# Moving the tail work of the next blocks and the weight splitting in a fused retention and FFN kernel

## The chip, the cores and the metric

The kernel runs on one core of a Trainium2 chip. A core has TensorE (PE) for matrix products, VectorE (DVE), ScalarE (ACT) and GpSimd (POOL) for elementwise work, and SyncE (SP), from which this kernel issues nearly all of its DMAs. The engines run side by side, each through its own list of instructions in order, and wait for each other through semaphores. The metric is the device time in microseconds (us); lower is better.

## The reference

Input x is 4 x 1024 tokens of 512 features, float32. Two layers, each between a norm and a residual:

```python
x = x + layernorm(attn(layernorm(x)))
x = x + layernorm(ffn(layernorm(x)))

# attn, with 16 heads of 32 features and a decay lam per head
q, v = x @ Wq.T, x @ Wv.T
ret[t] = lam * ret[t-1] + v[t]            # along each sequence
out = layernorm(q * ret) * gamma + beta
out = (out * silu(x @ Wg.T)) @ Wo.T

# ffn, weights rounded to fp8, with 1536 hidden features
gate = silu((x @ gate_w) * gate_scale)
up = (x @ up_w) * up_scale
out = ((gate * up) @ down_w) * down_scale
```

## The kernel before, in words

The 4096 tokens are cut into 8 blocks of 512, each of 4 tiles of 128 tokens. Weights stay in SBUF or come through a ring of four buffers (`w_ring`), filled by DMA from SP: each product that has used a buffer issues the fetch for the product four later (`fetch_weights`).

The main loop (L1238) runs over t, the block whose FFN is computed, and i from 0 to 11, the slices of 128 hidden features. Every step (t, i) has three large groups of matmuls: `f.gate(i)` (pfg), `f.up(i)` (pfu) and `f.down(i - 2)` (pd). Between them, work of other blocks is laid in by hand:

- `b`, the retention layer of block t + 1: its products fill the gaps (pv, pq, pg and, for the output matrix, po), followed by moments, residual and norm.
- `n`, the retention layer of block t + 2: its x tiles are loaded, normed and turned.
- `l`, the tail of the FFN of block t - 1.

Each step has a first part (before `f.up`), a middle ("mid", after `f.fuse`) and an end. Everything is recorded through `InOrder` (L66 to L74), which keeps program order on each engine, so the position of a line in the loop is its position in the engine's list. All instructions carry line 74 in the profile; they are told apart by tile names. A step at which one engine waits holds up whatever stands behind it on that engine.

For b of block 2 and 3 the products are of the seven-product kind: `product` (L665) runs them in the orders at L333 to L336 (for the output: 1, 2, 6, 5, 3, 7, 4) on half matrices, in two PSUM banks, and VectorE or ScalarE adds each bank to a part in SBUF (`mids`). Number 6, 7 and 4 of a kind use one bank in turn, so number 4 of the output can accumulate only when VectorE has read number 7's sum (`add_o`, L733). The output products of every later block are of this kind too.

From block 4 on (`by_parts`) the v, q and g products use split weights and a split x. A weight is split into its upper bits (top), the rest (low) and a combination (diff); x likewise:

- `Splitter` (L395) prepares the weights in 12 units (v, q, g, four column chunks each) during t = 1 and 2. Unit n has a load (`l`, two DMAs), a split (`s`, three VectorE instructions and one of GpSimd) and a store (`k`, two DMAs), placed by the table `times` (L431). A unit uses a pair of 128 x 512 buffers: two pairs lie in the freed room of the output weights, and unit 7 has one under the tag xn.
- `low_of(k)` (L570) and `diff_of(k)` (L585) split tile k of x, with two VectorE instructions and one.
- x reaches its turned form through DRAM: `norm_x` (ScalarE), `send_x` (a VectorE transpose of 32 x 32 blocks and a DMA to `mx`), and `fetch_x` (L554, four DMAs; in these blocks once for tiles 0 and 1 and once for tiles 2 and 3).

For the retention block b, `o_moments(s)` takes mean and variance of the output of tile s (VectorE, then GpSimd for the root), `x1_of(s)` norms it (ScalarE) and adds the residual (GpSimd), `x1_moments(s)` and `x1n_of(s)` norm the sum, and `move_x1n(s)` or `turn_x1n(s)` turn it for the FFN. `center_y` (L845) subtracts the mean from y on VectorE, and ScalarE squares the result.

Of the kernel before, what the change touches and what calls it, by code (L numbers as in the profile page):

```python
# [10 lines left out]
F32 = mybir.dt.float32  # L11
# [6 lines left out]
P = 128  # L18
# [5 lines left out]
def retention_ffn_sandwich(  # L24
# [20 lines left out]
    NT, D = x.shape  # L45
    I = gate_w.shape[1]
    NC = D // P
    NI = I // P
# [10 lines left out]
    work = ctx.enter_context(tc.tile_pool(name="work", bufs=2))  # L59
# [6 lines left out]
    class InOrder:  # L66


        def __init__(self, engine):
            self.engine = engine  # L70
# [324 lines left out]
    class Splitter:  # L395


        def __init__(self):
            room = wpool.tile([P, 4, D], F32, tag="wo_sb", name="split_room")
            self.pairs = [(room[:, 0], room[:, 1]), (room[:, 2], room[:, 3])]  # L400
            self.units = [(k, c) for k in "vqg" for c in range(NC)]
            self.sources = {"v": wvT, "q": wqT, "g": wgT}
            self.pair = {n: p if p is None else self.pairs[p] for n, p in enumerate((0, 1, 0, 1, 0, 1, 0, None, 1, 0, 1, 0))}

        def load(self, n):
            k, c = self.units[n]
            if self.pair[n] is None:
                room = work.tile([P, 2, D], F32, tag="xn", name=f"split_room_{n}", bufs=1)
                self.pair[n] = room[:, 0], room[:, 1]
            w = self.pair[n][0]  # L410
# [15 lines left out]
        def store(self, n):  # L426
# [2 lines left out]
            sp.dma_start(operands[k, c]["low"], w)  # L429

        times = {  # L431
# [6 lines left out]
        }  # L438

        def at(self, *when):  # L440
# [664 lines left out]
    a = Retention(0, x_first)  # L1105
# [20 lines left out]
    b = Retention(1)  # L1126
# [111 lines left out]
    for t in range(NB):  # L1238
        f, n = Ffn(a), None
        fast = b is not None and b.fast  # L1240
        for i in range(NI):
            if t > 0 and (t > 1 or i) and not (fast and i == 11):
                (f if i else l).rest((i - 1) % NI)
            if t == 0 and i == 0:
                n = Retention(2)
# [40 lines left out]
                b.gap(3 * i)  # L1286
            if fast and 7 <= i < 10:
                b.product()
            if n and n.by_parts and i == 7:
                n.norm_x(1, True)  # L1290
                n.send_x(1)
            if n and n.by_parts and i == 8:
                n.fetch_x(1)
                n.low_of(0)
                n.low_of(1)
            if n and n.by_parts and i == 9:
                n.diff_of(0)
                n.diff_of(1)
            if t == PARTS - 2 and i == 9:
                for _ in range(RING - 1):  # L1300
                    fetch_weights()
# [48 lines left out]
            if fast and i == 9:  # L1350
                b.x1_moments(0)
                b.x1_moments(1)
            if fast and i == 10:
                b.x1_of(2)
                b.x1_of(3)
# [20 lines left out]
            if t == 0 and i == 11:  # L1376
                b.upper_of(2)
            if fast and i == 9:
                loads = []
                for s in range(2):  # L1380
                    b.x1n_of(s, shift_scale)
                    loads.append(b.move_x1n(s))
                for load in loads:
                    load()
                if n and not n.by_parts:
                    n.input_sums(1, 2)
# [36 lines left out]
            if fast and i in (7, 8):  # L1423
                b.product()
            if n and n.by_parts and i == 7:
                n.norm_x(2, True)
                n.send_x(2)
            if n and t > 0 and i == 8 and not n.by_parts:
                n.fetch_x()
            if fast and i == 8:  # L1430
                b.o_moments(0)
                b.o_moments(1)
                b.x1_of(0)
                b.x1_of(1)
            if fast and i == 9:
                b.o_moments(2)
                b.o_moments(3)
            if fast and i == 10:
                b.x1_moments(2)
                b.x1_moments(3)  # L1440
# [28 lines left out]
            if b and not fast and i >= 9:  # L1469
                b.rest_of(i - 9)  # L1470
            if n and t > 0 and i in (6, 7):
                for s in ([0], [3] if n.by_parts else [1, 2])[i - 6]:
                    n.norm_x(s, True)
                    n.send_x(s)
            for _ in range(look[i][1] if t == 1 else 0):
# [66 lines left out]
            if t == 1 and i == 0:  # L1542
                output_sums()
                splitter = Splitter()
# [9 lines left out]
            if b and i == 4 and 0 < t < NB - 2:  # L1554
                n = Retention(t + 2)
# [4 lines left out]
        l, a, b = f, b, n  # L1560
# [67 lines left out]
```

## Time and profile before

| What | Value |
|---|---|
| Time, median of 3 runs | 984.98 us (984.90 to 985.68) |
| Profiled execution | 984.96 us, of which its span is 983.1 us |
| Busy: TensorE, VectorE, ScalarE, GpSimd | 952.1, 681.0, 442.2, 270.8 us |
| DMA | 148.14 MB, mean 151 GB/s |
| One splitting unit on VectorE, undisturbed | 0.42 + 0.69 + 0.69 us |
| One pair of moments on VectorE (two tiles) | 1.7 us |
| Time between two blocks' same steps, t = 3 to 5 | 116.3 us |

Rows of a timeline give the start and duration in us, the engine, the line, the operation, its output and inputs, the shapes, how many instructions are merged, and in brackets the idle time of the engine before it with what ended it. Rows of a waits view give the total, the number of times and the longest. Starts are counted from the start of the span. TensorE's matmul ends are modelled, so distances between starts are safer than idle times.

### The profile page before, as it was taken

To read this page: it belongs to the slowest core of one execution; us is meant where nothing else is said; L and a number is where in the kernel's file an instruction comes from. 1 tells how busy PE (TensorE), PEld (TensorE's weight loads), DVE (VectorE), ACT (ScalarE), POOL (GpSimd) and SP (SyncE) were. 2 spreads that over 40 slices of the span, in tenths; PEclk is the share of its full clock that TensorE was granted. 3 is DMA by queue.
4 is the path that set the end of the run, shared out by engine and by line. 5 is a ranking of instruction groups with operands and counts; after the bars stand their busy time and mean duration, and the time that the engine had idled before them with its cause. 6 is when DMAs were issued, how large, how long until landed. Compare 5 with 4: busy or idle time off the path is not lost.

```text
span 983.1 us, 11900 instructions
## 1 busy us (share of the span) xinstructions
PE 952.1 (97%) x4022; PEld 746.2 (76%) x4022; DVE 681.0 (69%) x1042; ACT 442.2 (45%) x709; POOL 270.8 (28%) x340
## 2 busy tenths in 40 slices
PE   9999999999899998999999999999999999999997
PEld 7456766687787877878878788887878778787885
DVE  5996999767776888875577745876457755646445
ACT  3556675467566115343353424435263332625223
POOL 1405121403327134240332305222052212314020
PEclk9999999999999999999999999999999999999999
DMA  9311424845728666456455464556463464514021
GB/s 305 113 61 56 141 65 108 247 148 179 237 88 238 222 225 232 167 146 190 140 186 150 135 188 149 162 159 183 141 199 111 146 206 140 152 52 128 2 86 43
DMA packets 115756, 148.14 MB, mean 151 GB/s; under 512 B 10352, under 2 KB 61040, under 8 KB 115696
## 3 DMA queue, kind: packets, MB, share of 16 engines
q1 hardware_dynamic: 114832, 146.72, 48.3%
q8 instruction: 32, 0.52, 0.2%
q10 hardware_dynamic: 864, 0.66, 0.2%
q14 instruction: 28, 0.23, 0.1%
HBM read 108.81 MB, written 42.47 MB: 154 GB/s over the span
## 4 chain that ended last, share of the span: by engine, by line
PE 63%; DVE 18%; ACT 7%; POOL 5%; issue 4%; DMA 3%; SPq 0%; DVEq 0%; POOLq 0%; ACTq 0%
PE pfg L74 11%; PE pfu L74 10%; PE pd L74 10%; PE pv L74 8%; PE po L74 8%; PE pq L74 8%; PE pg L74 6%; DVE st L74 3%; ACT x1n L74 2%; DVE split_room L74 2%; DVE y L74 2%; DVE fuse L74 2%; DVE gate L74 1%; POOL x L74 1%; DVE scr L74 1%
## 5 line engine op out<-in xcount | busy, mean ns | idle before, releaser
L74 PE MATMUL pfu<-x1nT,up_sb 128*128 128x512 f32 x768 | 200.7, 403 | 7.1 <-DVE gate L74 7.1
L74 PE MATMUL pfg<-x1nT,gate_sb 128*128 128x512 f32 x768 | 195.4, 396 | 0.9 <-DVE x1nT L74 0.4
L74 PE MATMUL pd<-down_sb,fuse 128*128 128x512 f32 x720 | 184.8, 398 | 0.0
L74 PEld LDWEIGHTS pfu<-x1nT,up_sb 128*128 128x128 f32 x768 | 143.6, 188 | 43.1 <-DVE gate L74 10.9
L74 PEld LDWEIGHTS pfg<-x1nT,gate_sb 128*128 128x128 f32 x768 | 143.7, 188 | 32.9 <-ACT gate L74 2.1
L74 PEld LDWEIGHTS pd<-down_sb,fuse 128*128 128x128 f32 x720 | 136.1, 189 | 28.1
L74 ACT CAST fuse<-gate 128x512 fp32r<-128x512 f32 x90 | 55.7, 619 | 198.7 <-DVE gate L74 198.6
L74 ACT ACTIVATE gate<-pfg,gs_sb 128x512 f32<-128x512 f32 x96 | 65.6, 683 | 96.5 <-PE pfg L74 96.5
L74 DVE SCALAR_TENSOR_TENSOR gate<-pfu,us_sb,gate 128x512 f32<-128x512 f32 x96 | 71.6, 745 | 51.5 <-PE pfu L74 47.2
L74 POOL TENSOR_SCALAR mv<-mv 128x1 f32<-128x1 f32 (+1 forms) x82 | 24.3, 297 | 273.7 <-DVE mv L74 270.6
L74 DVE TENSOR_TENSOR fuse<-gate,fuse 128x512 fp32r<-128x512 f32 x90 | 74.7, 830 | 5.5 <-ACT fuse L74 5.5
L74 DVE BATCH_NORM_STATS2 st<-x 128x6 f32<-128x512 f32 x64 | 43.6, 681 | 24.8 <-POOL x L74 22.2
L74 POOL TENSOR_TENSOR ysum<-y 128x512 f32<-128x512 f32 (+1 forms) x10 | 11.8, 1183 | 171.2 <-DVE y L74 171.2
L74 POOL TENSOR_TENSOR mv<-mv,nhalf 128x1 f32<-128x1 f32 (+1 forms) x75 | 50.2, 670 | 6.2
L74 POOL TENSOR_TENSOR x<-x,x1n 128x512 f32<-128x512 f32 x32 | 41.5, 1296 | 12.3 <-ACT x1n L74 12.0
L74 POOL TENSOR_TENSOR d<-d,x 128x512 f32<-128x512 f32 x28 | 37.1, 1348 | 18.6 <-ACT d L74 16.7
L74 DVE TENSOR_TENSOR mids<-po,mids 128x512 f32<-128x512 f32 x30 | 20.5, 684 | 28.7 <-PE po L74 28.4
L74 POOL TENSOR_TENSOR sqsum<-sqsum,sq 128x512 f32<-128x512 f32 x24 | 34.9, 1454 | 17.4 <-ACT sq L74 16.0
L74 DVE TENSOR_TENSOR y<-pq,y 128x512 f32<-128x512 f32 x18 | 12.5, 692 | 37.4 <-PE pq L74 37.4
L74 POOL TENSOR_TENSOR ysum<-ysum,y 128x512 f32<-128x512 f32 (+1 forms) x20 | 22.2, 1110 | 52.1 <-DVE y L74 51.8
L74 DVE RECIPROCAL rstd<-rstd 128x512 f32<-128x512 f32 x8 | 26.8, 3352 | 11.5 <-ACT rstd L74 11.4
L74 ACT ACTIVATE scr<-scr,neg_low 128x1024 f32<-128x1024 f32 x18 | 20.6, 1145 | 24.1 <-DVE scr L74 24.0
(199 smaller groups left out, 1640.9 us busy)
## 6 DMA issues: line engine op xcount, KB each, us to landing
kept<-x SPq DMA_DIRECT2D x32, 256.0 KB, 2.5
x<-kept SPq DMA_DIRECT2D x32, 256.0 KB, 4.2
x<-in_x SPq DMA_DIRECT2D x28, 256.0 KB, 3.9
out<-d SPq DMA_DIRECT2D x27, 256.0 KB, 2.0
xnT<-mx SPq DMA_DIRECT2D x32, 128.0 KB, 2.9
w_ring_parts<-dtop_v SPq DMA_DIRECT2D x16, 256.0 KB, 3.0
w_ring_parts<-dlow_v SPq DMA_DIRECT2D x16, 256.0 KB, 3.3
w_ring_parts<-ddiff_v SPq DMA_DIRECT2D x16, 256.0 KB, 3.1
```

Source lines behind the costliest of these rows:

```text
L74: return lambda *args, **kwargs: tc.keep_in_program_order(op(*args, **kwargs))
```

## The change

Five things are moved, and two buffer pairs added. The splitting units: other places in `times`, with a third moment in a step ("start", before the up projection), and pairs also under the tags xn (units 7 and 11) and ret (unit 8). In blocks with `by_parts`: the second `fetch_x` goes from the start of step 8 to the end of step 7; `low_of` of tiles 2 and 3 from the end of step 8 to its middle, in front of the moments of output tiles 0 and 1; `diff_of` of tiles 0 and 1 from the start of step 9 behind the moments of x1 there. In every block with a fast b: `x1n_of` of tiles 0 and 1 in front of the fuse of step 9, and the moments of output tiles 2 and 3 in front of the turns of x1n in step 9. The regrouping of `norm_x` for tiles 2 and 3 leaves the order on each engine as it was.

```diff
             room = wpool.tile([P, 4, D], F32, tag="wo_sb", name="split_room")
-            self.pairs = [(room[:, 0], room[:, 1]), (room[:, 2], room[:, 3])]
+            self.pairs = {"a": (room[:, 0], room[:, 1]), "b": (room[:, 2], room[:, 3])}
...
-            self.pair = {n: p if p is None else self.pairs[p] for n, p in enumerate((0, 1, 0, 1, 0, 1, 0, None, 1, 0, 1, 0))}
+            places = ("a", "b", "a", "b", "a", "b", "a", "xn", "ret", "b", "a", "xn")
+            self.pair = dict(enumerate(places))
...
+            elif place == "ret":
+                self.pair[n] = [
+                    work.tile([P, D], F32, tag="ret", name=f"split_room_{n}_{h}") for h in range(2)
+                ]
...
         times = {
-            (1, 1, "end"): "l0 l1", (1, 2, "mid"): "s0", (1, 2, "end"): "k0", (1, 3, "mid"): "l2 s1",
-            (1, 3, "end"): "k1", (1, 4, "mid"): "l3 s2", (1, 4, "end"): "k2", (1, 5, "mid"): "l4",
-            (1, 8, "mid"): "s3", (1, 8, "end"): "k3", (1, 9, "mid"): "l5 s4", (1, 9, "end"): "k4",
-            (1, 10, "mid"): "l6", (2, 0, "mid"): "l7 s5", (2, 0, "end"): "k5 s6", (2, 1, "mid"): "l8 s7 k6",
-            (2, 1, "end"): "l9 s8", (2, 2, "mid"): "k7 k8 s9", (2, 2, "end"): "l10 k9", (2, 3, "mid"): "l11 s10",
-            (2, 3, "end"): "k10", (2, 4, "mid"): "s11", (2, 4, "end"): "k11",
+            (1, 1, "end"): "l0 l1", (1, 2, "mid"): "s0", (1, 2, "end"): "k0", (1, 3, "mid"): "l2",
+            (1, 3, "end"): "s1", (1, 4, "mid"): "k1", (1, 4, "end"): "l3", (1, 7, "end"): "s2",
+            (1, 8, "mid"): "k2", (1, 8, "end"): "l4 s3", (1, 9, "mid"): "k3 s4", (1, 9, "end"): "k4 l5",
+            (1, 10, "end"): "l6 l7", (2, 0, "start"): "s5 l8", (2, 0, "mid"): "k5 s6", (2, 0, "end"): "k6 l9 s7",
+            (2, 1, "start"): "s8", (2, 1, "mid"): "k7 l10 s9", (2, 1, "end"): "k8 k9 l11",
+            (2, 2, "end"): "s10", (2, 3, "mid"): "k10", (2, 3, "end"): "s11", (2, 4, "mid"): "k11",
         }
...
+            if (1, 0) < (t, i) < (2, NI):
+                splitter.at(t, i, "start")
...
             if n and n.by_parts and i == 8:
-                n.fetch_x(1)
                 n.low_of(0)
                 n.low_of(1)
-            if n and n.by_parts and i == 9:
-                n.diff_of(0)
-                n.diff_of(1)
...
             if fast and i == 9:
                 b.x1_moments(0)
                 b.x1_moments(1)
+                b.x1n_of(0, shift_scale)
+                b.x1n_of(1, shift_scale)
+                if n and n.by_parts:
+                    n.diff_of(0)
+                    n.diff_of(1)
...
             if fast and i == 9:
+                b.o_moments(2)
+                b.o_moments(3)
                 loads = []
                 for s in range(2):
-                    b.x1n_of(s, shift_scale)
                     loads.append(b.move_x1n(s))
...
+            if n and n.by_parts and i == 8:
+                n.low_of(2)
+                n.low_of(3)
             if fast and i == 8:
                 b.o_moments(0)
                 b.o_moments(1)
                 b.x1_of(0)
                 b.x1_of(1)
-            if fast and i == 9:
-                b.o_moments(2)
-                b.o_moments(3)
...
-            if n and n.by_parts and i == 8:
-                n.low_of(2)
-                n.low_of(3)
+            if n and n.by_parts and i == 7:
+                n.fetch_x(1)
```

More of the change, by code (lines that the diff above doesn't have):

```diff
@@ L399, in __init__ @@
             room = wpool.tile([P, 4, D], F32, tag="wo_sb", name="split_room")
-            self.pairs = [(room[:, 0], room[:, 1]), (room[:, 2], room[:, 3])]
+            self.pairs = {"a": (room[:, 0], room[:, 1]), "b": (room[:, 2], room[:, 3])}
             self.units = [(k, c) for k in "vqg" for c in range(NC)]
             self.sources = {"v": wvT, "q": wqT, "g": wgT}
-            self.pair = {n: p if p is None else self.pairs[p] for n, p in enumerate((0, 1, 0, 1, 0, 1, 0, None, 1, 0, 1, 0))}
+            places = ("a", "b", "a", "b", "a", "b", "a", "xn", "ret", "b", "a", "xn")
+            self.pair = dict(enumerate(places))
         def load(self, n):
             k, c = self.units[n]
-            if self.pair[n] is None:
+            place = self.pair[n]
+            if place == "xn":
                 room = work.tile([P, 2, D], F32, tag="xn", name=f"split_room_{n}", bufs=1)
                 self.pair[n] = room[:, 0], room[:, 1]
+            elif place == "ret":
+                self.pair[n] = [
+                    work.tile([P, D], F32, tag="ret", name=f"split_room_{n}_{h}") for h in range(2)
+                ]
+            else:
+                self.pair[n] = self.pairs[place]
             w = self.pair[n][0]
@@ L1425, in retention_ffn_sandwich @@
             if n and n.by_parts and i == 7:
-                n.norm_x(2, True)
-                n.send_x(2)
+                for s in (2, 3):
+                    n.norm_x(s, True)
+                    n.send_x(s)
             if n and t > 0 and i == 8 and not n.by_parts:
                 n.fetch_x()
+            if n and n.by_parts and i == 8:
+                n.low_of(2)
+                n.low_of(3)
             if fast and i == 8:
@@ L1471, in retention_ffn_sandwich @@
             if n and t > 0 and i in (6, 7):
-                for s in ([0], [3] if n.by_parts else [1, 2])[i - 6]:
+                for s in ([0], [] if n.by_parts else [1, 2])[i - 6]:
                     n.norm_x(s, True)
```

## The prediction

> **What bounds the kernel now.** I read the page first, then the waits of TensorE, then the timelines of TensorE, VectorE, ScalarE, GpSimd and the DMA queue around each wait. Steps are (t, i): t is the FFN block, i one of its twelve steps. The page:
>
> ```profile
> span 983.1 us, 11900 instructions
> PE 952.1 (97%) x4022; PEld 746.2 (76%) x4022; DVE 681.0 (69%) x1042; ACT 442.2 (45%) x709; POOL 270.8 (28%) x340
> ```
>
> TensorE sets the time. The change leaves TensorE's own list of instructions untouched, so only its gaps can change. The view of its waits gives them:
>
> ```profile
> PE pfu L74 <- DVE gate L74: 7.1, 9, 1.4
> PE pg L74 <- ACT mids L74: 5.8, 2, 2.9
> PE pt L74 <- DVE x1n L74: 3.7, 7, 1.2
> PE pq L74 <- DVE mids L74: 1.9, 2, 1.2
> ```
>
> The two long pg waits are in steps (1,4) and (2,4). In TensorE's timeline (start, duration; in brackets the idle time before):
>
> ```profile
> 246.77 2.18 PE L74 MATMUL pfu<-x1nT,up_sb 128*128 128x512 f32 x8
> 251.84 2.67 PE L74 MATMUL pg<-t_sums,w_ring 128*128 128x256 f32 x8 [2.90 <-ACT mids L74]
> ...
> 377.43 1.99 PE L74 MATMUL pg<-t_sums,w_ring 128*128 128x256 f32 x8 [2.86 <-ACT mids L74]
> ```
>
> Each gap costs about 3.05 us (the next start should be 248.8 and 374.4). After the first, the granted clock falls to half (third column from the right):
>
> ```profile
> 253.00:256.40 3.40, 3.40 (x9) 2.68 (x8) 1.85 (x3) 2.50 (x4) 2.56 (x3) 0.50 0.21 33
> ```
>
> That costs another 1.7 us. The reason for the wait stands in VectorE's timeline: a splitting unit in front of the subtraction of the mean from y, whose squares ScalarE needs before its mids.
>
> ```profile
> 242.92 0.42 DVE L74 TENSOR_SCALAR split_room<-split_room 128x512 int32<-128x512 int32 x1
> 243.37 1.67 DVE L74 TENSOR_TENSOR split_room<-split_room 128x512 f32<-128x512 f32 x1
> 245.08 1.65 DVE L74 SCALAR_TENSOR_TENSOR split_room<-split_room 128x512 f32<-128x512 f32 x1
> 246.65 2.47 DVE L74 TENSOR_TENSOR y<-y,mu 128x512 f32<-128x512 f32 x4
> ```
>
> In blocks t = 2 to 5 the same three waits recur; in block 3:
>
> ```profile
> 546.92 2.11 PE L74 MATMUL pfu<-x1nT,up_sb 128*128 128x512 f32 x8 [0.48 <-DVE gate L74]
> ...
> 554.02 2.14 PE L74 MATMUL pfu<-x1nT,up_sb 128*128 128x512 f32 x8 [0.95 <-DVE gate L74]
> ...
> 560.66 0.66 PE L74 MATMUL pt<-ident,x1n 128*128 128x128 f32 x4 [0.39 <-DVE x1n L74]
> ```
>
> Against the undisturbed rhythm (an 8-matmul group starts 1.81 us after the one before) these steps lose 0.65 + 0.29 + 1.25 + 0.58, with 0.38 of slow restarts: 3.15 us in a block.
>
> **What the Trainium skill says.** SBUF — State Buffer, "Who interferes with whom": a VectorE instruction with two SBUF inputs and a GpSimd one that reads SBUF exclude each other. The trace agrees: the split's passes take 0.69 alone and 1.67 and 1.65 above, beside GpSimd's d additions (243.07 to 246.18); top and low of tile 2 take 1.24 and 1.68 at 538.1 beside the x additions, 0.42 and 0.69 elsewhere. TensorE: Matmul & The Clock Gate, "Part 1: The HAM clock gate": an idle window of about 3.4 us, free-running, halves the clock. The trace shows 3.4 us at 0.50 after one of two such gaps. The table at the head of that page calls VectorE's and ScalarE's queues strict FIFO; nothing above contradicts it.
>
> **The change part by part**
>
> *Splitting units, (1,3) and (2,3).* The unit now stands behind y - mu. For (2,4): y - mu runs from 369.15, not 372.24; the third square's buffer waits for GpSimd's first sqsum addition, which follows two d additions of 1.28 each (start 368.66) and so ends near 372.6, not 375.7. Square 0.63, gate 0.67, mids 0.59: mids ends near 374.4, when TensorE wants it. 3.05 us go. What is late next: the split, now beside the three sqsum additions, takes about 4 us, then fuse, gate, half. half ends near 380.3, and var on TensorE would now start at 379.75: about 0.6 comes back. Gain 2.4. In (1,4) the same with 0.3 left of the first wait and 0.7 at var, plus the clock's 1.7: 3.05 + 1.7 - 1.0 = 3.7.
>
> *Units at the end of block 1.* The unit in step 8 goes behind the o addition, into 2.12 us of idle time; nothing. In step 9 the two o moments (1.72) move in front of the turns, where VectorE idled 2.03 + 1.04, and the x1n norms pass the fuse cast on ScalarE. gate of step 10 then ends near 312.1 instead of 312.85: the wait of pfu 11 falls from 1.57 to 0.8, limited by the split beside GpSimd's t_sums. x1n 2 and 3 come 1 to 2 us earlier, so that pt's 0.6 goes. Gain 1.4.
>
> *SP's queue.* Load 5 reuses pair b and waits for store 3 to land (issued near 312, landing after 4.4 as the stores do at 313): the queue stands until about 316.5. Behind it are two kept stores, three copies of 1.95 in all, loads 6 and 7 (1.0 each). The weight fetch that went out at 321.17 goes out near 323.4; it took 5.6 to land there. Its product is at 329.32, minus the 1.4: 327.9. Stall between 0 and 1.6; I take 0.5.
>
> *Block 2, steps 0 to 2.* One more unit in front of gate in step 1 (two more by then, 1.77 each, one in 1.46 of idle time): gate at 343.9 instead of 341.9, so the copy of the first q product ends at 345.8, and the third q product (345.27) waits 0.6. In exchange the later unit is gone and the fifth q product's wait (1.36 at 353.74) falls away. Gain 0.7.
>
> *low of tiles 2, 3.* The heart of the matter, in t = 2 to 5. The four instructions (2.12 us) now stand in front of the o moments and of the addition for the sixth o product (number 7). They need the second xnT fetch, which SP can't issue earlier, since it waits for the x tiles' store to land. In block 3 it is issued 531.48 to 533.28 and the last part lands 3.8 after 532.83: 536.6. VectorE comes there at 534.6 and stands, with everything behind it. low to 538.8, two moments 1.7, the addition 0.7: 541.2. Before, that addition was here:
>
> ```profile
> 537.47 0.69 DVE L74 TENSOR_TENSOR mids<-po,mids 128x512 f32<-128x512 f32 x1 [1.12 <-PE po L74]
> ```
>
> and the last o product, which accumulates in the bank that it reads, follows close behind:
>
> ```profile
> 539.10 1.89 PE L74 MATMUL po<-w_ring_parts,y 128*128 128x256 f32 x8
> ```
>
> So a new wait of 2.1 us. By the landings the others are 2.7 (t = 2), 2.5 and 2.4, a mean of 2.4; I take off 0.1, as the dtop fetch no longer goes in front, and add 0.15 for the restart: 2.45. (gate 9 of ScalarE ends near 544.0, before pfg 10 at 546.6: no second wait.) What goes: after a delay of 2.45, gate of steps 9 and 10 end near 547.6 and 551.9 against wants of 548.4 and 554.0, x1n 3 likewise early; all 3.15 us go. Net 0.7, times four: 2.8. But gaps of 2.2 to 2.7 are near those of which one in two halved the clock; I count one of the four: -1.7. Net 1.1. No cover means here: each us by which xnT lands later costs 4 us in all.
>
> *Block 6.* No new loads. Moments 4 us earlier, the x1n norms 2 us: pt's 1.05, the start's 0.28 and pfg's 0.38 at 908.89 go. Gain 1.6 with restarts, less 0.1.
>
> *diff of 0 and 1 behind the x moments; the second unit in 2,4:* VectorE does them in time already counted.
>
> Sum: 3.7 + 2.4 + 1.4 - 0.5 + 0.7 + 1.1 + 1.5 = 10.3. The profiled execution took 984.96 around its span of 983.1 (1.86 outside it), the median is 984.98. 984.96 - 10.3 = 974.7.
>
> **Rivals.** (A) xnT lands sooner than in the profile (536.0 in block 3's time) and no clock drop: the new wait is 1.5, four blocks give 1.5 each, most of the residues at var and the late fetch go: 6.0 + 4.3 + 2.9 + 1.4 + 0.7 + 1.5 = 16.8, 968.2. For it: the dtop fetch is out of the way. Against: the wait for the store stays. (B) The splitting units' gain is taken by the next waits: var on half, the third q product and the late fetch (1.6) keep half of it: 2.7 + 1.0 + 0.7 - 1.6 + 0 + 1.1 + 1.0 = 4.9, 980.1. For it: VectorE is busy without a break from 329.6 to 342.7. (C) Slower: low of tile 2 waits long in all four blocks, and the gap halves the clock each time. The parts outside it give 9.2; so it decides from a loss of 2.8 in a block (2.3 to level, 0.5 for the bound): a wait of about 4.1 with the clock's 1.7, which means a landing 1.8 us later than now. With 2.5 us later: 4 x (4.95 - 3.15 + 1.7) = 14, less 9.2: 989.8. For it: landings of 5.6 occur at 321. Against: the xnT parts land after 2.5 to 3.8. (D) Nothing happens since the waits only change places: 984.
>
> **How the numbers follow.** Forecast (971 to 978) 0.5, A 0.17, B 0.17, C 0.12, D 0.04. Changes under 0.2% (2.0 us) can't be told from none. Faster: 0.5 + 0.17 + 0.17 = 0.84; same 0.04; slower 0.12. Range 967.5 to 984: it takes in A and B and leaves C and the tail of A out.
>
> **What would show it.** Right: no pg wait over 1 us on mids, no 0.50 clock near 253; a new wait "po from DVE mids" four times, 2 to 2.7 each; pfu on gate gone in t = 2 to 6; VectorE's top waiting for the DMA of xnT. Wrong: no such po wait (then A), waits of var and pq over 1 us (B), po waits over 4 with the clock at 0.50 (C).

## The result and the profile after

| | Median | Runs | Ratio to before, 95% interval |
|---|---|---|---|
| before | 985.05 us | 984.90 to 985.68 | |
| changed | 975.81 us | 974.44 to 976.66 | 0.9904 [0.9887, 0.9921] |

The changed kernel is 9.2 us faster; 974.7 was forecast. Its profiled execution took 975.05 around a span of 973.3, which is 9.8 us less than the span before. The page, after the change:

```profile
span 973.3 us, 11904 instructions
PE 948.2 (97%) x4022; PEld 745.0 (77%) x4022; DVE 677.3 (70%) x1042; ACT 442.5 (45%) x709; POOL 275.6 (28%) x340
```

TensorE has the same 4022 matmuls as before, so the 9.8 us can only come from gaps and from its clock. The view of its waits shows where the gaps went (total, times, longest):

```profile
PE po L74 <- DVE mids L74: 7.7, 4, 2.3
PE pfu L74 <- DVE gate L74: 1.6, 1, 1.6
PE pv L74 <- DVE total L74: 1.2, 1, 1.2
...
PE mu L74 <- ACT half L74: 0.7, 1, 0.7
```

The two pg waits (5.8) are gone, eight of the nine pfu waits too, and of pt's seven waits one is left (1.1, in block 0, as before). In their place stand four po waits, which the prediction had announced as "four times, 2 to 2.7 each" (they are 1.0 to 2.3); a pv wait at the start of block 2, which it had put at 0 to 1.6; and mu in (2,3), which it had not announced. Here mu and var are TensorE's products for the mean and the variance of y, fed by `half`, and pt are the turns of x1n.

TensorE's timeline at the two places where pg had waited 2.9 us, which now has no idle time in brackets:

```profile
245.32 2.18 PE L74 MATMUL pfu<-x1nT,up_sb 128*128 128x512 f32 x8
247.33 1.94 PE L74 MATMUL pg<-t_sums,w_ring 128*128 128x256 f32 x8
...
370.23 1.94 PE L74 MATMUL pg<-t_sums,w_ring 128*128 128x256 f32 x8
...
533.17 1.99 PE L74 MATMUL po<-w_ring_parts,y 128*128 128x256 f32 x8 [1.04 <-DVE mids L74]
...
540.45 1.98 PE L74 MATMUL pfu<-x1nT,up_sb 128*128 128x512 f32 x8
...
545.89 1.98 PE L74 MATMUL pfu<-x1nT,up_sb 128*128 128x512 f32 x8
```

The last three lines are block 3: one new wait at the last output product, and behind it both up projections of steps 10 and 11 on time. VectorE in (1,3) shows the reordering, with y minus the mean first and the splitting unit behind it:

```profile
242.14 2.48 DVE L74 TENSOR_TENSOR y<-y,mu 128x512 f32<-128x512 f32 x4 [0.59 <-PE mu L74]
244.53 1.25 DVE L74 TENSOR_SCALAR split_room<-split_room 128x512 int32<-128x512 int32 x1
245.82 1.67 DVE L74 TENSOR_TENSOR split_room<-split_room 128x512 f32<-128x512 f32 x1
247.52 1.65 DVE L74 SCALAR_TENSOR_TENSOR split_room<-split_room 128x512 f32<-128x512 f32 x1
...
644.55 0.43 DVE L74 TENSOR_SCALAR top<-xnT 128x512 int32<-128x512 int32 x1 [2.51 <-DMA xnT<-mx]
...
648.30 0.66 DVE L74 TENSOR_TENSOR mids<-po,mids 128x512 f32<-128x512 f32 x1
```

The last two lines are the origin of the po waits, here in block 4: VectorE stands 2.51 us for the second xnT fetch, and the addition that frees the bank of the last output product runs only at 648.30, behind low and two moments. In this block the clock then fell to half. Busy times by window (third column from the right is the granted clock); the second window follows the po wait of block 5, which was nearly as long (2.39 us from start to start, against 2.70) and had no such effect:

```profile
649.24:652.65 3.41, 3.41 (x9) 2.66 (x9) 0.32 (x2) 2.33 (x5) 3.23 (x3) 0.50 0.18 67
766.00:769.40 3.40, 3.16 (x14) 2.75 (x15) 1.91 (x4) 2.77 (x6) 3.30 (x4) 1.00 0.03 11
```

**Where the time went.** Since the order of TensorE's matmuls is the same in both kernels, each start of before can be set against the start of the same matmul after. The advance grows or shrinks at these places:

| Place | Forecast | Measured |
|---|---|---|
| step (1,4) with the clock | +3.7 | +4.0 |
| end of block 1 | +1.4 | +0.2 |
| late weight fetch, block 2 step 0 | -0.5 | -1.35 |
| block 2, steps 0 to 2 | +0.7 | +0.8 |
| mu in (2,3) | not in the sum | -1.1 |
| step (2,4) | +2.4 | +2.5 |
| blocks 2 to 5, with one clock drop | +1.1 | +1.7 |
| block 6 | +1.5 | +1.4 |
| one pq wait in block 1 | not in the sum | +0.9 |
| first 60 us (a start-up phase) | none | +0.6 |

The last two rows can't be put down to the change: the start-up phase moves by about 1 us between other pairs of kernels below, and at this pq product kernels whose program is the same up to there have 0.25 to 1.30 us from start to start. The rows add up to 9.7; the rest are shifts under 0.2 each.

### The profile page after: what moved, and what is told of

It reads as the page before. It is cut to its first block, busy times and chain, and to the rows that moved or that the text cites. A ratio compares the mean times of both kernels' runs of the same rounds, so it can differ in the third digit from the quotient of the medians.

```text
span 973.3 us, 11904 instructions
## 1 busy us (share of the span) xinstructions
PE 948.2 (97%) x4022; PEld 745.0 (77%) x4022; DVE 677.3 (70%) x1042; ACT 442.5 (45%) x709; POOL 275.6 (28%) x340
## 4 chain that ended last, share of the span: by engine, by line
PE 65%; DVE 15%; DMA 5%; POOL 5%; ACT 4%; issue 4%; SPq 1%; DVEq 0%; ACTq 0%; POOLq 0%
PE pfg L74 12%; PE pfu L74 12%; PE pd L74 11%; PE pv L74 9%; PE pq L74 8%; PE po L74 6%; PE pg L74 5%; DVE st L74 3%; DMA mx<-xn 2%; DVE y L74 2%; DVE split_room L74 2%; DVE fuse L74 1%; DMA xnT<-mx 1%; SPq L74 1%; DVE half L74 1%
## 5 line engine op out<-in xcount | busy, mean ns | idle before, releaser
L74 POOL TENSOR_TENSOR mv<-mv,nhalf 128x1 f32<-128x1 f32 (+1 forms) x75 | 53.1, 709 | 6.2
```

The lines of the kernel that those rows point to most:

```text
L74: return lambda *args, **kwargs: tc.keep_in_program_order(op(*args, **kwargs))
```

## Experiments

Times are medians; each ratio is to the kernel before, run beside it on the same chip. "Matched starts" means the comparison just used. A wait in brackets is idle time of TensorE; a gap "start to start" runs from one matmul's start to the next one's and is about 0.4 longer.

| Kernel | Median us | Ratio, 95% interval |
|---|---|---|
| splitting units alone | 979.63 | 0.9953 [0.9938, 0.9967] |
| moments and x1n norms alone | 974.71 | 0.9902 [0.9886, 0.9919] |
| changed, low back at the end of step 8 | 970.84 | 0.9851 [0.9834, 0.9867] |
| changed, low behind the moments | 975.43 | 0.9906 [0.9880, 0.9933] |
| changed, low in step 9 | 971.86 | 0.9878 [0.9854, 0.9903] |
| the same, kept stores later | 966.86 | 0.9814 [0.9799, 0.9829] |
| changed, units 1 and 11 in front of y - mu | 985.05 | 0.9997 [0.9982, 1.0012] |
| all mends, low in step 9 | 964.06 | 0.9787 [0.9772, 0.9802] |
| all mends, low at the end of step 8 | 965.99 | 0.9806 [0.9791, 0.9820] |
| changed, again | 976.59 | 0.9906 [0.9884, 0.9928] |

**1. The two halves of the change, each alone.** The first takes from the change only the table of the units, its pairs and the third moment of a step:

```diff
-            self.pairs = [(room[:, 0], room[:, 1]), (room[:, 2], room[:, 3])]
+            self.pairs = {"a": (room[:, 0], room[:, 1]), "b": (room[:, 2], room[:, 3])}
...
         times = {
...
+            (1, 3, "end"): "s1", (1, 4, "mid"): "k1", (1, 4, "end"): "l3", (1, 7, "end"): "s2",
...
+            if (1, 0) < (t, i) < (2, NI):
+                splitter.at(t, i, "start")
```

> The kernel before with the new table and pairs of the splitting units alone; low, moments, x1n, fetch and diff as before. From the matched starts of the two traces the units' share is +4.2 in (1,4), -1.35 at the late weight fetch, +0.8 in block 2 steps 0 to 2, -1.1 at mu in (2,3), +2.5 in (2,4), together +5 us: 979 to 981 us, no po wait, the pfu waits of 7 us and the pt waits still there. Rival (the end of block 1 is held up by the units there, and the moments' move hides it in the full change): pfu waits at the end of block 1 of 2 us or more beyond those before; 982 to 984 us.

Measured: 979.63, 4.3 us faster than the kernel beside it. The pg waits are gone by matched starts (+3.1 in each step, and about 1.4 of the clock in (1,4)); mu costs 1.1. But the rival has a part in it. TensorE at the end of block 1:

```profile
308.56 3.31 PE L74 MATMUL pfu<-x1nT,up_sb 128*128 128x512 f32 x8 [2.72 <-DVE gate L74]
```

The wait there grew from 1.42 to 2.72, and the clock halved behind it, 2.9 us lost in all. In the full change the moments in front of the turns take that back: its wait is 1.61. The number met the theory in part by luck: the late weight fetch, counted at -1.35, cost nothing here, since TensorE comes to it later by what it lost at pfu.

The second half moves the moments of output tiles 2 and 3 in front of the turns and the x1n norms of tiles 0 and 1 in front of the fuse, and nothing else:

```diff
             if fast and i == 9:
                 b.x1_moments(0)
                 b.x1_moments(1)
+                b.x1n_of(0, shift_scale)
+                b.x1n_of(1, shift_scale)
...
             if fast and i == 9:
+                b.o_moments(2)
+                b.o_moments(3)
                 loads = []
                 for s in range(2):
-                    b.x1n_of(s, shift_scale)
                     loads.append(b.move_x1n(s))
...
-            if fast and i == 9:
-                b.o_moments(2)
-                b.o_moments(3)
```

> The kernel before with only the moments of output tiles 2 and 3 in front of the turns of x1n in step 9 and the x1n norms of tiles 0 and 1 in front of the fuse. Theory (this part frees pfu 11 and pt; low at the end of step 8 still delays gate 10 by its 2.1 us, which leaves the 0.65 of pfu 10): about 2.3 us in each of four blocks, 1.4 in block 6, 1 to 2 at the end of block 1: 972 to 975 us, with pfu waits of some 2 us left and no pt waits. Rival (the moments alone bring nothing as long as low stands at the end of step 8, since gate 10 is late either way): 982 to 985 us.

Measured: 974.71, 9.2 us faster, as much as the whole change. TensorE's waits (dlow_v is the low part of the v weights in DRAM):

```profile
PE pg L74 <- ACT mids L74: 5.8, 2, 2.9
PE pfu L74 <- DVE gate L74: 1.8, 4, 0.5
PE pv L74 <- DMA w_ring_parts<-dlow_v: 1.7, 3, 0.8
```

The theory held: 2.1 to 2.35 us a block by matched starts (pfu 11 1.25, pt 0.6 to 0.7, the rest at pfg 11), 1.2 in block 6, 1.6 at the end of block 1, where the pfu wait is gone, and four short waits of pfu 10 are left, which low at the end of step 8 causes. The third line is new: three waits for a weight fetch, of which more below. The moments and the x1n norms were not tried apart, so their shares stay open.

The halves sum to 13.5 us and the whole brought 9.2, so the remaining part, which is mainly the place of low, should cost about 4.

**2. Low back at the end of step 8.**

```diff
-            if n and n.by_parts and i == 8:
-                n.low_of(2)
-                n.low_of(3)
             if fast and i == 8:
                 b.o_moments(0)
...
             if fast and i in (7, 8):
                 b.product()
+            if n and n.by_parts and i == 8:
+                n.low_of(2)
+                n.low_of(3)
```

> The changed kernel with low of tiles 2 and 3 back at the end of step 8; the fetch, diff, moments and x1n norms stay where the change put them. From the two halves of the change (units alone 4.3 us, moments alone 9.2 us faster than before, the whole change 9.2), the move of low would cost 4.3 us. Theory (the halves add up, low in the middle of step 8 is a loss): 970.5 to 973 us, no po waits, pfu 10 waits of about 0.4 in four blocks. Rival (the halves overlap, and each bought part of the same time): 974.5 to 977 us even without the po waits, with other waits in their place.

Measured: 970.84, ratio 0.9851 against 0.9904 for the change, and the intervals don't touch. The move of low was a loss of about 5 us inside a gain. Its waits for gate and for dlow_v:

```profile
PE pfu L74 <- DVE gate L74: 3.3, 5, 1.6
PE pv L74 <- DMA w_ring_parts<-dlow_v: 2.5, 4, 1.1
```

The matched starts give the loss as a sum. From this kernel to the changed one, the po gaps cost 2.5 + 1.1 + 2.3 + 2.0 and the clock 1.8: 9.7 us. In return four pfu 10 waits of 0.5 go (1.9), and so do the four waits for dlow_v (3.7), since a TensorE that has just stood 2 us asks for that weight later. Net 4.1. More than a third of the new stall's price is hidden, because it stands in front of another stall that it makes unnecessary. In block 3, for example, the fetch goes out at 549.64 in this kernel and at 549.89 in the changed one, but TensorE asks for it at 552.97 here and at 554.12 there. The gain with low back is 14 us, about what the two halves sum to, so the moves of the second `fetch_x` and of diff are worth little either way.

**3. What makes the po wait: the landing or the work?** One kernel puts the moments of tiles 0 and 1 in front of low, so that they fill the time in which VectorE stands; the other takes low out of step 8.

```diff
+            if fast and i == 8:
+                b.o_moments(0)
+                b.o_moments(1)
             if n and n.by_parts and i == 8:
                 n.low_of(2)
                 n.low_of(3)
             if fast and i == 8:
-                b.o_moments(0)
-                b.o_moments(1)
                 b.x1_of(0)
```

> In step 8 of blocks 2 to 5 the moments of output tiles 0 and 1 (1.7 us) stand in front of low of tiles 2 and 3, so that they fill the time in which VectorE stands for the second xnT fetch. Theory (the landing wait, with moments and number 7's addition queued behind it, makes the four po waits of 1.0 to 2.3 us): the po waits sum to 1 to 2 us in place of 7.7, the clock drop at 649 goes (1.7), the later waits of pfu 10 stay away; 969 to 972 us, 0.4 to 0.7% faster than the changed kernel. Rival (the amount of work in front of the addition makes it late, since low and moments together are 3.8 us in either order): the po waits stay near 7.7 in sum and the time near 975.8.

Measured: 975.43, the same as the change within the intervals, where the theory wanted 969 to 972. The profiled execution itself took 971.43, the others 975.17 to 977.78, and only the profiled one left a trace. In it three of the four po waits had shrunk to gaps of 0.34 to 0.45 start to start (0.23 is the rhythm), as the theory has it. In block 2 the wait had grown to 2.9, with the clock at half behind it, and VectorE shows a cause that neither side had named:

```profile
414.28 0.43 DVE L74 TENSOR_SCALAR top<-xnT 128x512 int32<-128x512 int32 x1 [0.90 <-DMA xnT<-mx]
414.75 0.69 DVE L74 TENSOR_TENSOR low<-xnT,top 128x512 fp32r<-128x512 f32 x1
415.36 1.51 DVE L74 TENSOR_SCALAR top<-xnT 128x512 int32<-128x512 int32 x1
416.91 1.63 DVE L74 TENSOR_TENSOR low<-xnT,top 128x512 fp32r<-128x512 f32 x1
418.46 0.68 DVE L74 TENSOR_TENSOR mids<-po,mids 128x512 f32<-128x512 f32 x1
```

GpSimd at that time:

```profile
414.77 3.22 POOL L74 TENSOR_TENSOR x<-x,x1n 128x512 f32<-128x512 f32 x2 [0.34 <-ACT x1n L74]
```

Earlier moments release the x additions on GpSimd earlier, and low now runs beside them: top and low of tile 3 take 3.14 us in place of 1.11. The Trainium skill says of this in SBUF — State Buffer, section "Who interferes with whom", that a VectorE instruction with two SBUF inputs and a GpSimd one that reads SBUF hold each other up; the trace agrees, with 0.69 alone and 1.63 beside. Whether this, or a late landing, also made the slower executions of this kernel can't be told. So the run shows that the landing makes the wait in three blocks, and does not show a gain from this order.

The other kernel:

```diff
-            if n and n.by_parts and i == 8:
-                n.low_of(2)
-                n.low_of(3)
...
             if fast and i == 9:
                 b.o_moments(2)
                 b.o_moments(3)
+                if n and n.by_parts:
+                    n.low_of(2)
+                    n.low_of(3)
                 loads = []
```

> low of tiles 2 and 3 moves from step 8 to step 9, behind the moments of output tiles 2 and 3 and in front of the turns of x1n. Theory (low at its place in step 8 costs its wait for the landing and gives nothing; all of the recovered 2.9 us per block comes from the moments in front of the turns and the x1n norms): no po waits, pfu 10 and 11 still without waits, 2.4 us per block in four blocks less than the changed kernel, and no drop of the clock at 649 (1.7): 964 to 967 us. Rival (it was low's leaving of the end of step 8, with 2.1 us less in front of gate 10, that freed step 10, so that low in step 9 gives the waits of pfu 10, pfu 11 or pt back): po waits gone, but 1.5 to 3 us of pfu and pt waits per block; 973 to 977 us.

Measured: 971.86 (970.11 to 975.22). The po waits are gone and pfu 10 and 11 are on time, so the rival falls: the place of low in step 8 gave nothing that step 9 doesn't give. But the forecast of 964 to 967 is missed by 5 us, because a third wait had stood behind both. TensorE in block 4:

```profile
664.25 1.11 PE L74 MATMUL pv<-xnT,w_ring_parts 128*128 128x512 f32 x4
666.78 1.19 PE L74 MATMUL pv<-low,w_ring_parts 128*128 128x512 f32 x4 [1.42 <-DMA w_ring_parts<-dlow_v]
```

and the DMA queue of SP before it:

```profile
658.90 1.54 SPq L74 DMA_DIRECT2D x1n<-mxs  x2
660.48 0.91 SPq L74 DMA_DIRECT2D kept<-x  x2
661.43 0.49 SPq L74 DMA_DIRECT2D w_ring_parts<-dlow_v  x1
```

The product that frees the buffer for this fetch is the one at 658.79, yet the fetch goes out at 661.43, behind the loads of x1n, which wait for the stores of the turns, and behind two stores of the residual that is read back only at 668.37.

**4. The kept stores later.** On top of the kernel just seen:

```diff
             if fast and i == 10:
-                b.x1_of(2)
-                b.x1_of(3)
+                b.x1_of(2, now=not (n and n.by_parts))
+                b.x1_of(3, now=not (n and n.by_parts))
...
             if n and i == 11:
                 n.gap(-2)
+                if fast and n.by_parts:
+                    b.keep(2)
+                    b.keep(3)
```

Here `keep(s)` is the store of the sum of tile s to `kept`, taken out of `x1_of(s)`.

> The kernel with low of tiles 2 and 3 in step 9 and, besides, the two stores of the kept x1 tiles 2 and 3 behind the first v products of step 11 in the DMA queue instead of in front of them. There the fetch of the second low part waits behind the x1n load and these two stores (0.9 us of issuing, and 0.5 MB of traffic beside its landing), and TensorE waits for it 1.0 to 1.6 us in four blocks. Theory (the queue's order makes the fetch late): the fetch goes out 0.9 us earlier and lands sooner, the pv waits sum to 0 to 1.5 us in place of 4.2; 967.5 to 970.5 us, and less spread than 970 to 975. Rival (the x1n load in front of it, which waits for eight stores, sets the issue): the waits stay above 3 us and the time within 971 to 973.

Measured: 966.86 (965.71 to 967.71), a ratio of 0.9814 against 0.9878, and less than half the spread; the time is a little below the theory's 967.5 to 970.5. The queue and the product in the same block:

```profile
659.35 1.56 SPq L74 DMA_DIRECT2D x1n<-mxs  x2
660.96 0.43 SPq L74 DMA_DIRECT2D w_ring_parts<-dlow_v  x1
...
661.91 1.65 SPq L74 DMA_DIRECT2D kept<-x  x2
```

```profile
664.72 1.11 PE L74 MATMUL pv<-xnT,w_ring_parts 128*128 128x512 f32 x4
665.66 1.07 PE L74 MATMUL pv<-low,w_ring_parts 128*128 128x512 f32 x4
```

The fetch now follows the product at 659.25 by 1.7 us instead of 2.6, and no dlow_v wait is left in any block: five us by the medians, 4.8 by the matched starts, from moving two stores that no wait names. The Trainium skill, DMA: Bandwidth & Descriptors, section "Anatomy of one DMA — SWDGE (gpsimd) path", says that a transfer's semaphore wait takes place at the issuing sequencer, ahead of dispatch. It says so of another path, but SP's queue here agrees: the fetch goes out only behind the issues in front of it, and 0.9 us of these were the two stores. The earlier issue is not all: from issue to landing this fetch took 4.6, 4.3, 5.3 and 5.2 us in the four blocks before, and 3.3, 4.3, 4.0 and 4.3 here. That it is the two stores' traffic which no longer slows it is likely, but no run shows it alone.

**5. Units 1 and 11 in front of y - mu again.**

```diff
-            (1, 1, "end"): "l0 l1", (1, 2, "mid"): "s0", (1, 2, "end"): "k0", (1, 3, "mid"): "l2",
-            (1, 3, "end"): "s1", (1, 4, "mid"): "k1", (1, 4, "end"): "l3", (1, 7, "end"): "s2",
+            (1, 1, "end"): "l0 l1", (1, 2, "mid"): "s0", (1, 2, "end"): "k0", (1, 3, "mid"): "l2 s1",
+            (1, 4, "mid"): "k1", (1, 4, "end"): "l3", (1, 7, "end"): "s2",
...
-            (2, 2, "end"): "s10", (2, 3, "mid"): "k10", (2, 3, "end"): "s11", (2, 4, "mid"): "k11",
+            (2, 2, "end"): "s10", (2, 3, "mid"): "k10 s11", (2, 4, "mid"): "k11",
```

> The changed kernel with units 1 and 11 back in front of the subtraction of the mean from y in (1,3) and (2,3). Theory (a unit there, slowed beside GpSimd, delays the squares and with them mids): both pg waits of some 2.9 us return, the small var waits after them go, and the clock may drop after the first again: 4.5 to 7.5 us slower than the changed kernel, 980 to 983 us. Rival (the gain in these steps came from other units being gone from steps 3 and 4, or from their loads and stores): no pg waits of more than 1 us, within 1.5 us of the changed kernel.

Measured: 985.05, 9.2 us slower than the change and more than the theory's 7.5. TensorE:

```profile
250.61 3.68 PE L74 MATMUL pg<-t_sums,w_ring 128*128 128x256 f32 x8 [2.90 <-ACT mids L74]
```

Both waits are back, of 2.90 each, 3.06 each by matched starts, so the order of the unit and the subtraction is their cause. What the theory had too small is the clock: in this profile three periods of half speed come, one here (about 1.5) and two in a row behind a po gap of 3.35 at 657 (3.1). The granted clock over a whole execution was 0.988 to 0.993 in nine of the twelve, against 0.994 to 0.998 for the change.

**6. The waits at mu and at the late weight fetch.** First unit 10, from the end to the middle of (2,2):

```diff
-            (2, 2, "end"): "s10", (2, 3, "mid"): "k10", (2, 3, "end"): "s11", (2, 4, "mid"): "k11",
+            (2, 2, "mid"): "s10", (2, 3, "mid"): "k10", (2, 3, "end"): "s11", (2, 4, "mid"): "k11",
```

> The changed kernel with unit 10 in the middle of (2,2) instead of its end. Theory (at the end it stands in front of the last d moments on VectorE and its scaling in front of the roots on GpSimd, so that mean of y comes late): the mu waits of 0.72 and 0.23 in (2,3) go, 1.1 us by the matched starts there. Rival (the mean is late because of the later q product, not of the unit): the mu waits stay.

One execution, 975.37, within the spread of the change. The place itself is clear. Before this edit the changed kernel's TensorE had

```profile
363.76 0.50 PE L74 MATMUL mu<-half,mean_r 128*128 128x512 f32 x1 [0.72 <-ACT half L74]
364.49 0.50 PE L74 MATMUL mu<-half,mean_r 128*128 128x512 f32 x1 [0.23 <-DVE half L74]
```

and with it

```profile
363.75 1.01 PE L74 MATMUL mu<-half,mean_r 128*128 128x512 f32 x2
```

without idle time, 1.0 us regained by matched starts. The unit at the end of the step stood in front of the last d moments.

Then the three copies of the output weights, which were in the queue in front of the late weight fetch:

```diff
-            if t == 1 and i == 10:
+            if t == 2 and i == 6:
                 copy_output_weights()
```

> The changed kernel with the three copies of the output weights issued at the end of (2,6) instead of (1,10). They take 2.2 us of the DMA queue's issuing in front of the weight fetch that went out at 318.78 there. Theory (the fetch is late by the queue): the fetch goes out about 2 us earlier and the pv wait of 1.2 at 325 falls to 0 to 0.3. Rival (its landing time or VectorE's total sets the wait): the wait stays above 0.8.

One execution, 978.32. The fetch went out at 317.36 in place of 318.78 and landed at 322.37 in place of 324.91, and the pv wait at 325 fell away, 1.4 us: the copies in front of it were the cause. 1.4 of these 2.5 us are the earlier issue, the rest is a shorter trip of the fetch. The other runs agree: with the copies at (1,10) and all units moved, this gap is 1.5 to 2.4 us from start to start in eight profiles, and 0.23 only in experiment 1's, where TensorE comes 2.9 later; it is 0.23 in all three with the copies elsewhere. The new place was worse than the old. The queue in step (2,6) and after:

```profile
397.35 1.89 SPq L74 DMA_DIRECT2D dcopy_o<-in_woT  x3
399.34 0.55 SPq L74 DMA_DIRECT2D w_ring<-in_woT  x1
...
406.10 1.80 SPq L74 DMA_DIRECT2D xnT<-mx  x4
```

The copies stand in front of an output weight's fetch, and beside the store that the xnT fetch waits for, which takes 6.0 us to land in place of 2.4; the xnT fetch goes out at 406.10 in place of 402.49. TensorE waits 1.54 at one output product and 4.26 at the last:

```profile
421.22 2.08 PE L74 MATMUL po<-w_ring,y 128*128 128x256 f32 x4 [4.26 <-DVE mids L74]
```

**7. All mends together.** Low in step 9, the kept stores later, unit 10 earlier; the copies from (1,10) to the end of (2,5), where the queue of the changed kernel issues nothing from 389.65 to 398.05; unit 4 split in step 10.

```diff
-            (1, 8, "mid"): "k2", (1, 8, "end"): "l4 s3", (1, 9, "mid"): "k3 s4", (1, 9, "end"): "k4 l5",
-            (1, 10, "end"): "l6 l7", (2, 0, "start"): "s5 l8", (2, 0, "mid"): "k5 s6", (2, 0, "end"): "k6 l9 s7",
+            (1, 8, "mid"): "k2", (1, 8, "end"): "l4 s3", (1, 9, "mid"): "k3", (1, 10, "mid"): "s4",
+            (1, 10, "end"): "k4 l5 l7", (1, 11, "mid"): "l6", (2, 0, "start"): "s5 l8", (2, 0, "mid"): "k5 s6", (2, 0, "end"): "k6 l9 s7",
...
             if t == 2 and i == 5:
                 store_late()
+                copy_output_weights()
```

> The kernel with low in step 9 and the kept stores later; unit 10 in the middle of (2,2); the copies of the output weights behind the late stores of (2,5), where the DMA queue is free from 389.7 to 396.9 and the traffic is small; unit 4 split in the middle of (1,10), loads 5 and 7 at its end, load 6 in the middle of (1,11). Theory: beyond the kernel with kept stores later, the mu waits (1.1), the pv wait at 325 (1.3) and the pfu wait at the end of block 1 (1.6) go: 963.5 to 966.5 us. Rival (unit 4 in step 10 delays gate 11 or the loads of units 5 and 6, and the copies delay the x transfers of block 2): 967 us or more, with new waits in block 2.

Measured: 964.06 (963.30 to 965.07), ratio 0.9787: 20.9 us faster than before, about 12 faster than the change. TensorE's two longest totals of waits, of which 1.2 of the first and all of the second are in block 0:

```profile
PE pt L74 <- DVE x1n L74: 2.4, 2, 1.2
PE pv L74 <- ACT xnT L74: 1.4, 2, 1.2
```

The pfu, pv and mu waits of blocks 1 and 2 have left the view. The rival was right in one point: unit 4 in step 10 delays x1n of tile 3 there, and pt waits 1.21 at the end of block 1, so that of the 1.8 regained at pfu 1.3 is lost again. From the step-9 kernel with later stores the matched starts gain 1.8 at pv, 1.0 at mu and 0.5 at the end of block 1. The same with low at the end of step 8 (the edit of experiment 2 in place of that of step 9):

> The same collection with low of tiles 2 and 3 at the end of step 8 in place of step 9. Theory (low at the end of step 8 costs 0.57 in front of gate 10 in each of four blocks, and nothing else): 2 us more than with low in step 9, 965.5 to 968.5 us, with four pfu waits of about 0.4. Rival (the time of low is free in either place): within 0.7 us of the kernel with low in step 9.

Measured: 965.99, 1.9 more, with four pfu waits of 0.4 and 0.57 to 0.6 a block in the matched starts. The theory held.

**8. The changed kernel once more.**

> The changed kernel itself, once more, beside the others: 974.4 to 977 us as in its first runs; po waits of 1 to 2.9 us in four blocks, with the clock drop behind another of them than at 649, or none, if it depends on the length of the gap.

Measured: 976.59 (973.49 to 977.82). The po gaps at the same four matmuls were 2.24, 1.60, 2.42 and 2.24 start to start (2.73, 1.43, 2.70 and 2.39 the first time), and the clock fell behind the last of them, at 766, not behind the longer one at 650.

## Why the prediction was right, and where not

The forecast was 974.7 and the result 975.81, and most of it came from the sum that it was built on. That it lies so close is in part luck: three terms fell short by 3.2 us together (the end of block 1, the late fetch, mu), and 1.5 us came back from the pq wait and the start-up, which can't be put down to the change, and 1.0 from terms that were a little better than forecast.

*Splitting units in (1,3) and (2,3): right.* 3.7 was forecast and 4.0 measured, 2.4 and 2.5; at var 0.4 and 0.5 come back, where 0.7 and 0.6 were forecast, and the clock was worth 1.4, not 1.7. Experiment 5 puts the waits back by the order alone.

*End of block 1: wrong, by a term put at nothing.* The pfu 11 wait was to fall from 1.57 to 0.8, counted from start to start; it is 1.76 (1.99 less the rhythm of 0.23), and with 0.4 gained at pt the place brings 0.2 in place of 1.4. The step that failed is "The unit in step 8 goes behind the o addition, into 2.12 us of idle time; nothing." Before, VectorE waited there for TensorE:

```profile
297.83 0.68 DVE L74 TENSOR_TENSOR fuse<-gate,fuse 128x512 fp32r<-128x512 f32 x1
300.63 0.69 DVE L74 TENSOR_TENSOR mids<-po,mids 128x512 f32<-128x512 f32 x1 [2.12 <-PE po L74]
```

In the changed kernel unit 3 fills the idle time, and GpSimd adds x beside it (292.98 to 296.22), so that the unit's last pass takes 1.65 in place of 0.69 and the fuse behind it 1.78 in place of 0.68:

```profile
293.42 1.65 DVE L74 SCALAR_TENSOR_TENSOR split_room<-split_room 128x512 f32<-128x512 f32 x1
294.99 1.78 DVE L74 TENSOR_TENSOR fuse<-gate,fuse 128x512 fp32r<-128x512 f32 x1
296.69 0.68 DVE L74 TENSOR_TENSOR mids<-po,mids 128x512 f32<-128x512 f32 x1
...
306.85 0.74 DVE L74 SCALAR_TENSOR_TENSOR gate<-pfu,us_sb,gate 128x512 f32<-128x512 f32 x1
```

```profile
307.65 2.12 PE L74 MATMUL pfu<-x1nT,up_sb 128*128 128x512 f32 x8 [1.61 <-DVE gate L74]
```

The addition starts 3.43 after its product (po at 293.26), before 1.92 (po at 298.71): 1.5 us late, and everything behind it on VectorE too. With the moments alone (the second half in experiment 1), where unit 3 stands at its old place, the addition starts 1.92 after the product again, and pfu 11 loses 0.27; from there to the end of gate VectorE takes 10.9 us in both. Unit 4, which the forecast had as the limit, is slowed beside t_sums in both alike (1.37 + 1.66 + 0.69 here, 1.35 + 1.67 + 0.69 there), so it does not make the difference. With the units alone the addition is as late (3.44), without the moments' gain. No run moves unit 3 by itself; experiment 7 takes unit 4 out from behind it, and the pfu wait goes.

*Late weight fetch: the range held, the value didn't.* 0 to 1.6 was given and 0.5 taken; it was 1.35. The copies in front of the fetch are the cause that experiment 6 shows, and the forecast had them in the queue.

*mu in (2,3): missed.* "In exchange the later unit is gone" counted what moves out of (2,2)'s middle, not what the unit at its end now stands in front of: the last d moments and through them half. 1.1 us.

*Blocks 2 to 5: right, and it held the real finding back.* Four po waits with VectorE's top waiting for the DMA were forecast at a mean of 2.45 with one clock drop; measured 2.1 with one drop. Recovered were 3.0 a block, against 3.15. What the text did not ask is what low's place would be worth without the moments' move. Experiments 1 and 2 answer: the moments alone bring as much as the whole change, 9.2, and low's move takes 4 to 5 of a possible 14 back. It also said that each us of later landing costs 4 us in all. Experiment 2 shows that this is not so at first: the next limit, the dlow_v fetch, hides the first 0.3 to 1.2 us in each block.

*Block 6 and steps 0 to 2 of block 2: right* (1.4 and 0.8). The three waits named for block 6 add up to 1.7, where the text has 1.6.

*The rivals.* A (968.2, xnT landing sooner) did not come: po stood 1.0 to 2.3. B (980.1) has its seed at var, pq and the late fetch, which took 0.4 and 0.5, 0.4 and 1.35, but not half of the gain. C (989.8) needed waits of 4.1; the copies in step (2,6) of experiment 6 made one of 4.3, with the clock at half behind it, so the mechanism exists, and the change did not set it off. D is out.

## What to carry to other kernels

Cost every part of a change against the others as well as against the old kernel: a part that recovers a lot can carry one that loses, and the sum still looks like a success. A stall that is removed uncovers the next one in its shadow, so ask of every recovered stretch which transfer is only in time because of it, and what stands in front of that transfer in the queue. Work placed in an idle slot of VectorE costs its duration beside whatever GpSimd does there, which here was up to twice that alone, and it can slow what stands behind it as well: unit 3 fitted a slot of 2.12 us by its 1.8 us alone and made the next addition 1.5 us late. Moving one thing earlier can release the neighbour earlier too.

## Hardware behaviour that was not expected

*When a gap halves the clock.* Over all fourteen profiles, from 200 to 905 us, TensorE's gaps (start to start) between 1.6 and 2.2 us were 21, and none was followed by half speed. Those of 2.2 us or more were 23, and 10 were followed by it, starting between 0.6 us before the end of the gap and 1.2 us after. Length alone does not decide: 3.25, 3.27, 3.29 and 3.11 went without, 2.24 and 2.70 with. The same kernel has it at 649 in one execution and at 766 in another.

The place of the gap does. In each of these profiles the clock also falls near the end of the kernel, and the starts of half speed in one execution lie whole multiples of 3.413 us apart: 253.02 and 980.06 before (213 of them), 649.24 and 970.09 after the change (94), 766.25 and 971.05 in experiment 8 (60). If the span is divided into windows on that grid, half speed from a window's end on followed every gap with 2.23 us or more inside that window, except one with 2.25, and no gap with 2.07 or less in any window. The change's 2.73 at 418.56 is cut by a boundary at 417.13 into 1.31 and 1.43, and the clock stayed; the 2.24 at 766 in experiment 8 lay whole in one window, and the clock fell. So, as an estimate from these figures, whether a gap of some 2.3 to 4.4 us costs the clock depends on where it falls. The Trainium skill, TensorE: Matmul & The Clock Gate, "Part 1: The HAM clock gate", describes a window of 3.4 us that runs freely, which fits. The page asks for a whole idle window, and 2.24 us of one did it here; the measurement decides. Each such period, 3.41 us long, cost 1.4 to 1.8 us, and the one double period 3.1.

*Both sides pay.* Where passes of a split ran beside additions of GpSimd, they went from 0.42 to between 1.25 and 1.51 (the bit mask, with one input), and from 0.69 to between 1.63 and 1.67 (two inputs), and two x additions of GpSimd went from 2.54 (at 307.49, after the change) to 3.24 (at 292.98).
